# A fused attention kernel: normed tiles, a square root and projections put in another order between two attention layers

## The chip, the cores and the metric

The kernel runs on one core of one Trainium2 chip. A core has five engines that take instructions from queues of their own and wait for each other through semaphores: TensorE (PE, matrix products), VectorE (DVE, elementwise work and statistics), ScalarE (ACT, copies and activation functions), GpSimd (POOL) and SyncE (SP, which issues transfers). Products land in PSUM, which this kernel uses as eight banks of 128x512 fp32.

The metric is the device time of one execution in microseconds (us). The median of three runs of the kernel before is 2324.17 us (2321.87 to 2325.84).

## The reference

Eight images of 32x32 pixels and 384 channels go through two layers. Cut to what matters:

```python
# layer 0
x = x + conv_attention(group_norm(x))       # q, k, v; 6 heads; relative positions; softmax; projection
# layer 1
t = x.reshape(8, 1024, 384)
t = t + attention(layer_norm(t))            # one head of 384, causal
t = t + ffn(layer_norm(t))                  # sign weights, absmax quantization; changes five of eight images
```

The place of the change is the seam between the layers: the projection of layer 0 with its residual, the layer norm of each token (subtract the mean of its 384 channels, divide by the root of their variance plus 1e-5), and the query and value products of layer 1's attention:

```python
out = out @ proj_w + proj_b                 # end of layer 0's attention; x = x + out
m, s = mean(t, -1), var(t, -1)
n = (t - m) / sqrt(s + 1e-5)                # layer norm
scores = (n @ Wq) @ (n @ Wk).T              # the kernel multiplies Wq and Wk.T out once
v = n @ Wv
```

## The kernel before, in words

The images are worked on one after the other (order 5, 0 to 4, 6, 7). Within an image, the tokens lie as eight tiles of 128 (j = 0 to 7), in two halves of four. All of an image stays in SBUF between the stages.

At the seam, `attend0_fast` has left the attention output `oT` (channels on partitions). `project` multiplies one tile of it with the projection weights: three products of 384 columns, each two instructions in the trace. `begun` holds the projections of tiles 0 to 3, issued already; `more(j)` adds a projection to the residual `xt` on DVE (L975), and for j of 4 and more issues the projection first.

`normed` makes the layer norm of one half: per tile `bn_stats` and `bn_aggr` on DVE (L463, L464), then for the four tiles together an addition on DVE (L466), the square root on ACT (L467), a reciprocal on DVE (L469), and the four normed tiles `xn` on DVE (L474). It is a generator, so that its caller can do other things between its parts. `turn_normed` transposes the normed tiles on PE (L414, three transposes a tile) and copies them on ACT to `lnT` (L415).

The query and value products are made by a scheme with fewer multiplications than the plain one: a 384x384 product over 256 tokens is put together from 15 products of 128x128 blocks (`ProductSet`). There are four sets an image: queries and values of half 0 (here 1q_0 and 1v_0), then of half 1 (1q_1 and 1v_1). `sum_forms` first makes eleven sums of blocks of `lnT` on DVE (L568). `ProductSet.run` then issues the products in the order of `PROD_ORDER` into six PSUM banks A to F. Bank A gets six products and bank B five; after most of them ACT copies the partial sum out (L623, `keep`), and the next product into the same bank waits for this copy. POOL subtracts some copies from each other (L643, `PROD_COMBINE`), and DVE puts the finished blocks together (`put_queries` L1050, `put_values` L1055), which also frees a bank.

The order on an engine is the order of issue, changed where the text asks for it: `behind_of(ins)` and `tc.issue_after(ins)` put what stands under them behind the named instruction. `last_ended` carries such an instruction for DVE, `last_product` for PE. In the kernel before the text runs: `more` for tiles 0 to 6 and half 0's norm and transposes, with the statistics of half 1's first three tiles let in; half 0's forms; the last projection, its statistics and half 1's root and normed tiles; set 1q_0; half 1's transposes; 1v_0, 1q_1, 1v_1, one whole set after the other; then the scores of layer 1 (L1115).

## Time and profile before

| what | value |
|---|---|
| median of three runs | 2324.17 us |
| the profiled execution's own time | 2325.5 us |
| its span, first to last instruction | 2323.8 us |
| PE busy | 2282.9 us, 98% of the span |
| DVE busy | 1614.3 us, 69% |
| ACT busy | 1206.0 us, 52% |
| POOL busy | 525.3 us, 23% |
| mean granted PE clock | 0.992 |
| PE's waits for ACT in set 1q | 19.3 us, 8 times |

Busy time is the time in which an engine works on an instruction. The granted clock is the share of PE's full clock that the chip let through. The chain of waits follows the last instruction back to what released it. A timeline lists start, duration, engine, line and operation, and in brackets the idle time before an instruction with what ended it. In the timelines one `lsd` is the sum of variance and 1e-5 or its root, `lrs` the reciprocal, `xn` a normed tile, `pj` a projection, `pt` a transposed tile, `xf` a form and `u_1q` a copied partial sum.

### The profile page before, as it was taken

How to read it: one execution, taken by the hardware profiler on the slowest of the kernel's cores; microseconds unless marked ns; L12 is line 12 of the kernel's file. 1: busy time of each engine (PE TensorE's matmuls, PEld its weight loads, DVE VectorE, ACT ScalarE, POOL GpSimd, SP SyncE). 2: the span in 40 equal slices, each digit the busy share in tenths (PEclk: the TensorE clock that was granted, in tenths of full speed). 3: DMA queues.
4: the chain of work that ended last, by engine and by line, in shares of the span. 5: the costliest groups of instructions: out<-in, count | busy, mean ns of one | idle time of the engine just before them, and what ended most of it. 6: DMA issues, size and time to landing. Idle time of an engine off the chain costs nothing.

```text
span 2323.8 us, 30196 instructions
## 1 busy us (share of the span) xinstructions
PE 2282.9 (98%) x10739; PEld 1395.7 (60%) x10739; DVE 1614.3 (69%) x2703; ACT 1206.0 (52%) x2181; POOL 525.3 (23%) x690
## 2 busy tenths in 40 slices
PE   8999999999999999999999999999999999999998
PEld 4547554768645677547685466874477754755464
DVE  6887578775887548886468875578854788637872
ACT  4644266337663457644376543766444765326631
POOL 6412222230140401312202313013040131221310
PEclk9999999999999999999999999999999999999999
DMA  7520552040730115510308202063002362017100
GB/s 181 154 82 28 156 134 64 13 178 28 147 98 28 52 58 116 130 55 1 109 28 188 57 28 105 30 144 103 28 16 93 101 136 64 1 51 158 37 1 29
DMA packets 154137, 186.57 MB, mean 80 GB/s; under 512 B 110917, under 2 KB 123578, under 8 KB 151162
## 3 DMA queue, kind: packets, MB, share of 16 engines
q1 hardware_dynamic: 135600, 113.87, 19.9%
q0 software_dynamic: 17184, 69.22, 9.6%
q8 instruction: 88, 1.44, 0.3%
q10 hardware_dynamic: 1194, 1.45, 0.2%
q14 instruction: 71, 0.58, 0.1%
HBM read 83.24 MB, written 50.92 MB: 58 GB/s over the span
## 4 chain that ended last, share of the span: by engine, by line
PE 95%; DVE 4%; DMA 1%; issue 0%; ACT 0%; ACTq 0%; DVEq 0%
PE f_s L889 15%; PE f_av L915 14%; PE f_s L1115 8%; PE f_av L1130 8%; PE f_y L1290 7%; PE f_y L1240 7%; PE f_qk L558 5%; PE f_s L893 4%; PE f_pr_A L558 4%; PE f_pj L504 4%; PE f_pr_B L558 3%; PE f_pr_1q_A L558 2%; PE f_rel L558 2%; PE f_pr_1v_A L558 2%; PE f_pr_1v_B L558 2%; PE f_pr_1q_B L558 2%
## 5 line engine op out<-in xcount | busy, mean ns | idle before, releaser
L900 ACT ACTIVATE f_pr<-f_s 128x512 f32<-128x512 f32 x768 | 413.1, 595 | 41.4 <-PE f_s L893 36.8
L889 PE MATMUL f_s<-f_q,f_k 64*128 64x512 f32 x1536 | 399.1, 595 | 0.0
L907 DVE TENSOR_TENSOR f_sum<-f_sum,f_pr 128x1024 f32<-128x1024 f32 x288 | 362.9, 1260 | 23.5 <-DVE seen L545 0.8
L915 PE MATMUL f_av<-f_pr,f_v 128*64 128x512 f32 x1536 | 339.3, 594 | 0.0
L893 PE MATMUL f_s<-f_r,unit 64*128 64x512 f32 x768 | 308.0, 793 | 0.0
L915 PEld LDWEIGHTS f_av<-f_pr,f_v 128*64 128x64 f32 x1536 | 106.2, 137 | 196.4 <-issue 191.9
L889 PEld LDWEIGHTS f_s<-f_q,f_k 64*128 64x128 f32 x1536 | 145.9, 186 | 124.1 <-issue 66.3
L1115 PE MATMUL f_s<-f_q,f_lnT 128*128 128x512 f32 (+3 forms) x576 | 198.3, 488 | 0.0
L1130 PE MATMUL f_av<-f_v,f_pr 128*128 128x385 f32 x576 | 195.3, 486 | 0.0
L780 POOL DMA_DIRECT2D f_r<-f_far x192 | 102.1, 534 | 380.1 <-DVE f_far L774 179.9
L1130 PEld LDWEIGHTS f_av<-f_v,f_pr 128*128 128x128 f32 x576 | 108.3, 190 | 77.2 <-issue 11.5
L1124 ACT ACTIVATE f_pr<-f_s 128x512 f32<-128x512 f32 (+3 forms) x96 | 47.0, 490 | 204.3 <-DVE f_s L1120 161.5
L1115 PEld LDWEIGHTS f_s<-f_q,f_lnT 128*128 128x128 f32 x576 | 100.8, 190 | 70.3 <-issue 46.9
L1251 DVE TENSOR_REDUCE am<-f_h 128x1 f32<-128x1024 f32 (+2 forms) x80 | 71.6, 946 | 95.6 <-ACT f_h L1244 95.6
L1244 ACT ACTIVATE f_h<-f_y,biases 128x256 f32<-128x256 f32 x240 | 100.7, 471 | 67.0 <-PE f_y L1240 67.0
L905 DVE TENSOR_TENSOR f_sum<-f_pr,f_pr 128x1024 f32<-128x1024 f32 x48 | 66.5, 1385 | 92.9 <-ACT f_pr L900 92.9
L893 PEld LDWEIGHTS f_s<-f_r,unit 64*128 64x128 f32 x768 | 75.2, 187 | 89.7 <-issue 89.2
L558 PE MATMUL f_qk<-f_gnT,wq_sb 128*128 128x512 f32 x288 | 127.8, 595 | 0.0
L504 PE MATMUL f_pj<-wproj_sb,f_oT 128*128 128x384 f32 x384 | 127.3, 488 | 0.0
L1290 PE MATMUL f_y<-f_w2a,f_hilo 128*128 128x384 f32 x640 | 127.2, 341 | 0.0
L963 ACT COPY f_oT<-f_av 128x512 f32<-128x512 f32 x40 | 23.4, 585 | 193.9 <-PE f_av L915 193.9
L1290 PEld LDWEIGHTS f_y<-f_w2a,f_hilo 128*128 128x128 f32 x640 | 112.5, 188 | 3.8 <-issue 1.4
(272 smaller groups left out, 4081.2 us busy)
## 6 DMA issues: line engine op xcount, KB each, us to landing
f_far<-f_far SPq DMA_DIRECT2D x48, 512.0 KB, 4.9
f_r<-f_far SPq DMA_DIRECT2D x192, 128.0 KB, 2.8
f_r<-f_far POOLq DMA_DIRECT2D x192, 128.0 KB, 4.6
f_far<-f_far SPq DMA_DIRECT2D x192, 64.0 KB, 4.7
f_x<-in_x SPq DMA_DIRECT2D x32, 384.0 KB, 8.4
f_gnT<-in_xT SPq DMA_DIRECT2D x21, 512.0 KB, 4.6
f_w1a<-w1s POOLq DMA_DIRECT2D x5, 1536.0 KB, 6.7
f_w2a<-w2s POOLq DMA_DIRECT2D x5, 1536.0 KB, 9.1
```

The costliest lines, as they stand in the source:

```text
L504: nc.tensor.matmul(ps[:, :C], xT[:, k, ts(j, P)], w[:, k, cols], start=(k == 0), stop=(k == NC - 1))
L558: last_product[0] = nc.tensor.matmul(*args, **kw).ins
L780: put = (nc.gpsimd if i else nc.sync).dma_start(out=r(part, p).bitcast(F32).rearrange("(m i) t -> i m t", i=4)[2 * i + d], in_=pages[i][ts ...
L889: nc.tensor.matmul(sc[par], k[rows[par], p, ts(c, P)], q[rows[par], p, ts(half, 512)], start=True, stop=False)
L893: last_matmul[0] = nc.tensor.matmul(sc[par], unit[rows[par], c // 2 % 2].rearrange("i h w -> i (h w)"), r(2 * (c // 4) + c % 2, p)[rows[pa ...
L900: last_exp[0] = nc.scalar.activation(pr[:, ts(par, 512)], sc[par], AF.Exp).ins
L907: adds.append(nc.vector.tensor_tensor(total, total, pr, ALU.add).ins)
L915: last_matmul[0] = nc.tensor.matmul(av[ts(par, HD), :], v[:, c, ts(2 * p + par, HD)], pr[:, ts(par, 512)], start=(c == 0), stop=(c == NJ - 1),
L1115: last_score[0] = nc.tensor.matmul(sc[:, lo:], xT[:, c // 4, k, ts(c % 4, P)], q[:, half, k, lo:], start=(k == 0), stop=(k == NC - 1),).ins
L1130: nc.tensor.matmul(av[:, : C + 1], prs[c][:, ts(j - c, P)], v[:, c, :], start=(c == 0), stop=(c == j))
L1240: nc.tensor.matmul(ps, w1k[i // 2][:, ts(m, P)], xs[i % 2][:, half, i // 2, :], start=(i == 0), stop=(i == 2 * NC - 1))
L1290: nc.tensor.matmul(ps[:, :C], h, w, start=(i == 0), stop=(i == len(products) - 1))
```

## The change

Five edits, all in the branch for the fast path:

- `normed` gives control back after every tile's statistics and once more after the addition, so that ACT's root can be issued later than DVE's part. It also records its DVE instructions in `last_normed`.
- `more` only adds; the projections of tiles 4 to 7 are issued by a new `begin`.
- Half 0's four normed tiles are issued on DVE straight after half 0's statistics, ahead of tile 4's addition. The statistics of tiles 5 to 7 stand behind half 0's forms.
- On PE half 0's transposes stand between the projections of tiles 5 and 6 (before: between 6 and 7).
- The root of half 1 stands on ACT behind the eighth copy of set 1q_0 (before: ahead of the first). Half 1's transposes stand ahead of 1q_0's last product, and each of the first products of 1q_1 and 1v_1 stands ahead of the last product of the set before.

In the built program these are the only differences of order on PE; DVE, ACT and POOL differ in the same stretch alone, and SP does not differ. Which PSUM bank and which page of SBUF a tile gets is different in this stretch: half 1's third and fourth transposed tiles lie in the banks that D and E of 1q_0 had, in both kernels, and so wait for DVE's first two `put_queries`.

```diff
@@ normed
             for i, j in enumerate(js):
-                if i == 3:
-                    yield
                 st = pools.small.tile([P, 6], F32, tag="lst", name=f"lst_{name}_{j}")
                 nc.vector.bn_stats(st, xt[:, j, :])
-                nc.vector.bn_aggr(mv[:, i, :], st)
+                last_normed[0] = nc.vector.bn_aggr(mv[:, i, :], st).ins
+                yield
             sd = pools.small.tile([P, 4], F32, tag="lsd", name=f"lsd_{name}_{half}")
-            nc.vector.tensor_scalar_add(sd, mv[:, :, 1], 1e-5)
+            last_normed[0] = nc.vector.tensor_scalar_add(sd, mv[:, :, 1], 1e-5).ins
+            yield
             nc.scalar.activation(sd, sd, AF.Sqrt)
...
@@ attend0_fast
+            def begin(j):
+                begun[j] = project(wproj_sb, slice(0, C), oT, j, f"pj_{b}_{j}")
+
             def more(j):
-                ps = begun[j] if j < 4 else project(wproj_sb, slice(0, C), oT, j, f"pj_{b}_{j}")
-                nc.vector.tensor_tensor(xt[:, j, :], ps, xt[:, j, :], ALU.add)
+                nc.vector.tensor_tensor(xt[:, j, :], begun[j], xt[:, j, :], ALU.add)
...
@@ attention1
-            for j in range(7):
-                more(j)
-            layer_norm_T(xt, xT, 0, f"1_{b}")
             if pools.fast:
+                begin, more = more
+                for j in range(4):
+                    more(j)
+                *_, (tiles, _) = normed(xt, 0, f"1_{b}")
+                tiles = list(tiles)
+                begin(4)
+                norm = normed(xt, 1, f"1_{b}")
+                with behind_of(last_normed[0]):
+                    more(4)
+                    next(norm)
                 last_ended[0] = last_normed[0]
-                norm = normed(xt, 1, f"1_{b}")
-                next(norm)
+                begin(5)
+                turn_normed(xT, 0, tiles)
+                begin(6)
+                begin(7)
                 forms = forms_of(0)
                 with behind_of(last_ended[0]):
-                    more(7)
+                    for j in range(5, NJ):
+                        more(j)
+                        next(norm)
+                    next(norm)
+                last_ended[0] = last_normed[0]
+                of_q, of_v = products(0, forms)
+                of_q.run(10)
+                with behind_of(last_ended[0]), behind_of(of_q.last_copy):
                     tiles, _ = next(norm)
                     tiles = list(tiles)
                 last_ended[0] = last_normed[0]
-                first = products(0, forms)
-                next(first)
+                of_q.run(4, put_queries(0))
                 with behind_of(last_product[0]):
                     turn_normed(xT, 1, tiles)
                 last_product[0] = last_transpose[0]
+                of_q.run(1)
                 forms = forms_of(1)
-                next(first, None)
-                second = products(1, forms)
-                next(second)
+                of_v0, (of_q, of_v) = of_v, products(1, forms)
+                of_v0.run(14, put_values(0))
+                of_q.run(1)
+                of_v0.run(1)
+                of_q.run(13, put_queries(1))
+                of_v.run(1)
+                of_q.run(1)
                 queries_ended[0] = last_ended[0]
-                next(second, None)
+                of_v.run(14, put_values(1))
```

More of the change, by code (lines that the diff above doesn't have):

```diff
@@ L970, in attend0_fast @@
             with behind_last():
-                begun = [project(wproj_sb, slice(0, C), oT, j, f"pj_{b}_{j}") for j in range(4)]
+                begun = {j: project(wproj_sb, slice(0, C), oT, j, f"pj_{b}_{j}") for j in range(4)}
+            def begin(j):
+                begun[j] = project(wproj_sb, slice(0, C), oT, j, f"pj_{b}_{j}")
             def more(j):
-                ps = begun[j] if j < 4 else project(wproj_sb, slice(0, C), oT, j, f"pj_{b}_{j}")
-                nc.vector.tensor_tensor(xt[:, j, :], ps, xt[:, j, :], ALU.add)
-            return xt, more
+                nc.vector.tensor_tensor(xt[:, j, :], begun[j], xt[:, j, :], ALU.add)
+            return xt, (begin, more)
         def attend0_general(residual, b, q, k, r, v, later):
@@ L1025, in attend0_general @@
             pipelined([(j, h) for j in range(NJ) for h in range(NH)], scores, values)
-            return xt, lambda j: None
+            return xt, None
         def attention1(xt, more, b, between, start):
@@ L1045, in forms_of, with put_queries, put, put_values @@
                 return sum_forms(f"1_{b}_{half}", lambda k, n: xT[:, half, k, ts(1 - n, 256)], 256, nc.vector, True)
-            def products(half, forms):
-                def put_queries(ps, kept, p, n, op):
+            def put_queries(half):
+                def put(ps, kept, p, n, op):
                     return nc.vector.tensor_tensor(q[:, half, p, ts(1 - n, 256)], ps, kept, op).ins
-                def put_values(ps, kept, p, n, op):
+                return put
+            def put_values(half):
+                def put(ps, kept, p, n, op):
                     ps, kept = (t.rearrange("t (j c) -> t j c", j=2) for t in (ps, kept))
@@ L1055, in put_values, with products @@
                     return nc.vector.tensor_tensor(v[:, j : j + 2, ts(p, P)], ps, kept, op).ins
-                ProductSet(f"1q_{b}_{half}", forms, w1f[:, :, 0, :], 256, eng=nc.gpsimd).run(N_PROD, put_queries)
-                yield
-                of_v = ProductSet(
+                return put
+            def products(half, forms):
+                return ProductSet(f"1q_{b}_{half}", forms, w1f[:, :, 0, :], 256, eng=nc.gpsimd), ProductSet(
                     f"1v_{b}_{half}", forms, w1f[:, :, 1, :], 256, lambda x: [x[:, ts(j, P)] for j in range(2)], eng=nc.gpsimd
                 )
-                of_v.run(N_PROD, put_values)
-            for j in range(7):
-                more(j)
-            layer_norm_T(xt, xT, 0, f"1_{b}")
             if pools.fast:
+                begin, more = more
[8 more added lines that the diff above has]
+                    next(norm)
                 last_ended[0] = last_normed[0]
-                norm = normed(xt, 1, f"1_{b}")
-                next(norm)
+                begin(5)
+                turn_normed(xT, 0, tiles)
+                begin(6)
+                begin(7)
                 forms = forms_of(0)
                 with behind_of(last_ended[0]):
-                    more(7)
+                    for j in range(5, NJ):
[6 more added lines that the diff above has]
+                with behind_of(last_ended[0]), behind_of(of_q.last_copy):
                     tiles, _ = next(norm)
@@ L1081, in attention1 @@
                 last_product[0] = last_transpose[0]
+                of_q.run(1)
                 forms = forms_of(1)
-                next(first, None)
-                second = products(1, forms)
-                next(second)
+                of_v0, (of_q, of_v) = of_v, products(1, forms)
[5 more added lines that the diff above has]
+                of_q.run(1)
                 queries_ended[0] = last_ended[0]
-                next(second, None)
+                of_v.run(14, put_values(1))
             else:
-                more(7)
+                layer_norm_T(xt, xT, 0, f"1_{b}")
                 layer_norm_T(xt, xT, 1, f"1_{b}")
```

## The prediction

> **What bounds the kernel now.** I read the chain of waits first, then PE's waits, then the timelines of the seam between the layers in the fifth image, and the granted clock in windows.

> Chain of waits, shares by engine; PE's longest wait:

> ```profile
> PE 95%; DVE 4%; DMA 1%; issue 0%; ACT 0%; ACTq 0%; DVEq 0%
> ...
> PE f_pr_1q_A L558 <- ACT f_u_1q L623: 19.3, 8, 2.4
> ```

> PE is the bound. What can be won is PE's idle or slow time, and its largest wait comes once an image, in set 1q_0. PE's timeline there (fifth image):

> ```profile
> 1364.91 2.10 PE L504 MATMUL f_pj<-wproj_sb,f_oT 128*128 128x384 f32 x6
> 1366.85 0.59 PE L558 MATMUL f_pr_1q_A<-f_xf,w1f 128*128 128x256 f32 x2
> 1367.71 0.70 PE L558 MATMUL f_pr_1q_B<-f_xf,w1f 128*128 128x256 f32 x2 [0.27 <-DVE f_xf L568]
> 1368.50 0.70 PE L558 MATMUL f_pr_1q_C<-f_xf,w1f 128*128 128x256 f32 x2
> 1371.61 0.70 PE L558 MATMUL f_pr_1q_A<-f_xf,w1f 128*128 128x256 f32 x2 [2.41 <-ACT f_u_1q L623]
> ```

> The second product of A waits for ACT's copy of the first. ACT stands at half 1's root, which waits for DVE (both timelines):

> ```profile
> 1370.89 0.17 DVE L466 TENSOR_SCALAR lsd<-lmv 128x4 f32<-128x4 f32 x1
> ...
> 1371.10 0.20 ACT L467 ACTIVATE lsd<-lsd 128x4 f32<-128x4 f32 x1 [5.34 <-DVE lsd L466]
> 1371.21 0.35 ACT L623 COPY f_u_1q<-f_pr_1q_A 128x256 f32<-128x256 f32 x1
> ```

> The wait has a second price. In the fourth image the products behind it start 0.85 us apart; in the fifth 0.43. PE's timeline and the windows (the seventh number, counts in brackets aside, is the clock):

> ```profile
> 1057.35 1.22 PE L558 MATMUL f_pr_1q_A<-f_xf,w1f 128*128 128x256 f32 x2 [2.41 <-ACT f_u_1q L623]
> 1058.36 1.06 PE L558 MATMUL f_pr_1q_B<-f_xf,w1f 128*128 128x256 f32 x2
> ...
> 1050.00:1060.00 10.00, 7.23 (x26) 4.76 (x25) 8.28 (x24) 3.24 (x10) 0.10 (x1) 0.81 0.00 0
> 1060.00:1070.00 10.00, 9.97 (x58) 8.59 (x57) 4.96 (x13) 5.23 (x14) 2.86 (x5) 0.85 0.00 1
> ```

> From the first projection to the first score takes 50.03, 51.39, 51.44, 51.37, 48.56, 48.55, 50.24 and 50.13 us in the eight images. Above 48.56 that is 13.2 us in all: the slow clock's cost. Ahead of 2310 us every 10 us window with a clock below 1.00 lies at this seam.

> [...] two forms take 1.70 us beside two POOL subtractions, 0.88 without:

> ```profile
> 1368.02 0.88 DVE L568 TENSOR_TENSOR f_xf<-f_xf,f_lnT 128x256 f32<-128x256 f32 x2
> ...
> 1381.59 1.70 DVE L568 TENSOR_TENSOR f_xf<-f_xf,f_lnT 128x256 f32<-128x256 f32 x2
> ```

> For `xn` beside POOL this trace has no case (all 104 take 0.456 to 0.481 us).

> **The change, part by part**, on the fifth image's clock. Instructions and transfers stay the same in number; SP's and POOL's order too, so no queue is passed.

> *Loss before.* Set pitch is 0.43 us a product for queries, 0.447 for values. From 1q_0's first product (1366.85) to the first score (1398.51) are 31.66 us. Needed: 15x0.4315 + transposes 1.32 + 15x0.4467 + 15x0.4315 + 14x0.4467 = 27.2. The loss is 4.43: B 0.43 and C 0.36 late for their forms, the wait 2.68, refilling 0.11, and 0.29, 0.27, 0.29 where the last product of 1q_0, 1v_0, 1q_1 waits for the copy just before it. Eight times 4.43 is 35.4 us; with the clock 48.7 us are at stake.

> *Half 0 early.* A root that is ready comes 0.44 us after its addition (1370.89 to 1371.33): reciprocal at 1359.84, xn 0 at 1360.05, pitch 0.38, so xn 3 ends at 1361.65 (before: 1363.3). Projections take 1.95 us each, so PE reaches the transposes at 1361.65: no wait, and 1q_0 begins at 1366.85 as before, since the same work is only reordered. ACT's copies follow the transposes by 0.53 and last 1.63: 1362.2 to 1363.8. Tile 4's addition and statistics end at 1362.9, so the forms start at about 1363.1 instead of 1365.09, take 4.4, and B and C don't wait: 0.79 won.

> *Root behind the eighth copy.* The first copies follow their products by 0.63, as in the later sets, so 2.68 + 0.11 go. What is late next? The forms end at 1367.5; three additions (pitch 0.47), three statistics and aggregations follow, in the row's pitches: `lsd` at 1370.9. The eighth copy starts at 1366.85 + 9x0.4315 + 0.64 = 1371.4, the root at 1371.63: 0.5 us of cover. Behind it stand copies nine (due 1371.80) and ten: not delayed. Reciprocal 1371.86, xn 4 at 1372.08, pitch 0.40, xn 7 at 1373.27, first put (D) 1373.67 to 1374.10.

> *The new wait.* PE would begin half 1's transposes at 1366.85 + 14x0.4315 = 1372.9. The third needs D's bank at 1373.55, but gets it at 1374.13: 0.58 us. POOL's subtraction for n3 (0.72 us) starts at 1371.82, just before xn 4: if it blocks it, 0.46 more. That for n6 falls on xn 5 to 7: up to 0.72 more. So 0.58 to 1.76; I take 1.3, one block and half of the other, plus 0.11 for refilling: 1.4. Queued behind D are E, F, C, B and A: the fourth transpose (E) follows 0.33 later without more wait, C is back before 1v_0's third product.

> *Set overlap.* One foreign product (0.43) stands before each last product, and covers 0.27 and 0.29; the transposes cover 1q_0's 0.29. Half 1's forms begin about 0.9 us later against 1v_0, but are wanted only 6.2 us after its start: covered.

> *Sum.* 4.43 - 1.4 = 3.03 an image, 24.2 us. If the slow clock goes too, 13.2 more: 37.5. The profiled execution's 2325.5 (span 2323.8) becomes 2288.0; the median stands 1.3 lower: **2287 us**.

> **Rivals.**
> (a) *The seam stays in the slow clock.* The new wait stands among transposes: from 1372.9 to 1375.6 PE has about 1.3 us of transposes and 1.4 of idleness. [...] For it: six of eight images after 2.41 us. Against: 1.4 us of idleness is little over half of that. All kept: 2324.2 - 24.2 = 2300; half kept 2293.
> (b) *Half 1's statistics are late.* DVE works 9.70 us of the ten from 1360 to 1370, and its cover is 0.5 us. 1.5 us late would push root, copies nine and ten and the transposes by 1 us more, and the clock goes slow: 2300 + 8 = 2308.
> (c) *Slower.* The root now stands ahead of copies nine and ten, so every delay of `lsd` past 1371.6 stops bank B, and PE, one for one. It decides where `lsd` comes 6.1 us (48.7 / 8) after its slot, at 1377.5; at 7 us the time is 2324 + 7 = 2331. The page has no DVE wait near that.
> (d) *No change:* only if new waits eat all; the order on ACT does show the root moved.

> **How the numbers follow.** Likeliest case 0.60: 2287, its own range 2280 to 2293 (wait 0.58 to 2.0). (a) 0.24; (b) 0.10; (c) 0.04; (d) 0.02. Faster than 0.2%, about what a measurement of this kernel can tell from no change, are the first three: 0.94. No residual at all would be 2324.2 - 48.7 = 2275.5, no block 2281: low end 2278. High end: slow clock kept and a wait of 2.0, 2304.

> **What would show it.** Right: no wait of 1q's A for the copies; granted clock 1.00 at the seam; a wait of about 1 us at half 1's third transpose, put down to DVE's put; first projection to first score about 45.5 us in each image. Wrong: distances of 0.85 behind the transposes (a); a wait of B in 1q_0 for copy nine and ACT idle for `lsd` (b, c); xn of 0.46 us beside POOL (then 2283).

## The result and the profile after

| | before | after |
|---|---|---|
| median | 2323.02 us (2321.37 to 2325.84, 4 runs) | 2286.43 us (2285.97 to 2286.72, 4 runs) |
| span of the profiled execution | 2323.8 us | 2284.7 us |
| mean granted PE clock | 0.992 | 0.999 |
| first product to first score, per image | 31.66 us at full clock, up to 34.54 | 28.45 or 28.46 us |
| the same, sum of eight images | 266.55 us | 227.63 us |

The ratio is 0.9841, with a 95% interval of 0.9824 to 0.9858. The kernel became faster by 36.6 us; 2287 was forecast. The seam accounts for the gain: 266.55 - 227.63 = 38.9 us, against 39.1 us of difference between the spans. Of these, 8 x (31.66 - 28.45) = 25.7 us are waits that went, net of the new one, and 266.55 - 8 x 31.66 = 13.3 us are the slow clock, which after doesn't show in any image's seam.

After's chain of waits by engine:

```profile
PE 98%; DVE 1%; DMA 1%; ACTq 0%; issue 0%; ACT 0%; DVEq 0%
```

PE's share rose from 95% to 98% and DVE's fell from 4% to 1%. The longest entry of PE's waits (total, times, longest):

```profile
PE f_pt L414 <- DVE f_q L1051: 7.8, 8, 1.0
```

The wait of 19.3 us for ACT's copies is gone. In its place PE waits 0.97 us an image at half 1's transposes. PE's timeline in the fifth image, whose first product of 1q_0 is now at 1343.87 (before: 1366.85):

```profile
1343.87 0.59 PE L558 MATMUL f_pr_1q_A<-f_xf,w1f 128*128 128x256 f32 x2
1344.30 0.59 PE L558 MATMUL f_pr_1q_B<-f_xf,w1f 128*128 128x256 f32 x2
...
1345.16 0.59 PE L558 MATMUL f_pr_1q_A<-f_xf,w1f 128*128 128x256 f32 x2
...
1349.91 0.86 PE L414 MATMUL f_pt<-ident,f_xn 128*128 128x128 f32 x6
1351.75 0.88 PE L414 MATMUL f_pt<-ident,f_xn 128*128 128x128 f32 x6 [0.97 <-DVE f_q L1051]
1352.46 0.60 PE L558 MATMUL f_pr_1q_A<-f_xf,w1f 128*128 128x256 f32 x2
```

From A's first product to its second are 1.29 us, three steps of 0.43; before they were 4.76. The transposes of tiles 4 and 5 start at 1349.91; those of tiles 6 and 7 could follow 0.66 us later but start 1.84 us later: a loss of 1.18 us, of which the profile counts 0.97 as idle.

ACT, DVE and POOL in the same stretch of after:

```profile
1347.86 0.44 DVE L465 TENSOR_SCALAR lsd<-lmv 128x4 f32<-128x4 f32 x1
1348.39 0.37 ACT L623 COPY f_u_1q<-f_pr_1q_A 128x256 f32<-128x256 f32 x1 [0.49 <-PE f_pr_1q_A L558]
1348.66 0.21 ACT L467 ACTIVATE lsd<-lsd 128x4 f32<-128x4 f32 x1
1348.84 0.73 POOL L643 TENSOR_TENSOR f_u_1q<-f_u_1q 128x256 f32<-128x256 f32 x1 [0.56 <-ACT f_u_1q L623]
1348.90 0.18 DVE L469 RECIPROCAL lrs<-lsd 128x4 f32<-128x4 f32 x1 [0.60 <-ACT lsd L467]
1349.11 2.25 DVE L474 TENSOR_SCALAR f_xn<-f_x,lmv,lrs 128x384 f32<-128x384 f32 x4
...
1350.19 0.96 POOL L643 TENSOR_TENSOR f_u_1q<-f_u_1q 128x256 f32<-128x256 f32 x1 [0.62 <-POOL f_u_1q L643]
...
1351.28 0.41 DVE L1051 TENSOR_TENSOR f_q<-f_pr_1q_D,f_u_1q 128x256 f32<-128x256 f32 x1
```

ACT now runs the root behind a copy, not ahead of one. The four normed tiles take 2.25 us beside POOL's two subtractions, and D's put (DVE's last step for bank D, which frees the bank) comes behind them; PE starts again 0.06 us after its end (1351.69).

### The profile page after: what moved, and what is told of

Read it like the earlier page. It is cut to its first block, busy times and chain, and to the rows that moved or that the text cites. A ratio compares the mean times of both kernels' runs of the same rounds, so it can differ in the third digit from the quotient of the medians.

```text
span 2284.7 us, 30195 instructions
## 1 busy us (share of the span) xinstructions
PE 2258.8 (99%) x10739; PEld 1387.6 (61%) x10739; DVE 1629.5 (71%) x2703; ACT 1210.5 (53%) x2181; POOL 527.2 (23%) x690
## 4 chain that ended last, share of the span: by engine, by line
PE 98%; DVE 1%; DMA 1%; ACTq 0%; issue 0%; ACT 0%; DVEq 0%
PE f_s L889 15%; PE f_av L915 14%; PE f_s L1139 8%; PE f_av L1154 8%; PE f_y L1314 7%; PE f_y L1264 7%; PE f_pj L504 5%; PE f_qk L558 5%; PE f_s L893 4%; PE f_pr_A L558 4%; PE f_pr_B L558 3%; PE f_rel L558 2%; PE f_pr_1v_A L558 2%; PE f_pr_1q_A L558 2%; PE f_pr_1v_B L558 2%; PE f_pr_1q_B L558 1%
## 5 line engine op out<-in xcount | busy, mean ns | idle before, releaser
L558 PE MATMUL f_qk<-f_gnT,wq_sb 128*128 128x512 f32 x288 | 127.8, 595 | 0.0
L504 PE MATMUL f_pj<-wproj_sb,f_oT 128*128 128x384 f32 x384 | 127.3, 488 | 0.0
```

Of the source, the lines that this page charges most:

```text
L504: nc.tensor.matmul(ps[:, :C], xT[:, k, ts(j, P)], w[:, k, cols], start=(k == 0), stop=(k == NC - 1))
L558: last_product[0] = nc.tensor.matmul(*args, **kw).ins
```

## The experiments

The theory: the gain is the root's move with the slow clock it caused, plus the earlier forms and the covered last products, less a new wait that hangs on DVE's chain from root to D's put. The rivals: the gain came from the other edits, or transposes and idleness together may keep the slow clock. Half 0's earlier tiles were not tried alone; what they do is read from the timeline. "Per image" below is the time from the first product of 1q_0 to the first score, at full clock; after has 28.45 us.

| run | median us | ratio to before (95%) | per image, us | slow clock in all, us |
|---|---|---|---|---|
| root back | 2314.05 | 0.9938 (0.9922 to 0.9955) | 30.73 | 9.2 |
| root alone | 2295.77 | 0.9866 (0.9849 to 0.9882) | 29.63 | 0 |
| last product first | 2283.75 | 0.9813 (0.9797 to 0.9829) | 28.07 | 0 |
| banks before puts | 2285.88 | 0.9821 (0.9804 to 0.9837) | 28.45 | 0 |
| whole later sets | 2291.36 | 0.9847 (0.9828 to 0.9866) | 29.03 | 0 |
| root behind tenth copy | 2291.46 | 0.9849 (0.9829 to 0.9868) | 29.05 | 0 |
| no subtractions | 2281.66 | 0.9805 (0.9786 to 0.9824) | 27.85 | 0 |
| put in the gap | 2280.29 | 0.9801 (0.9782 to 0.9820) | 27.74 | 0 |
| every wait | 2281.01 | 0.9820 (0.9804 to 0.9836) | 27.74 | 0 |
| long wait | 2325.36 | 1.0005 (0.9996 to 1.0014) | 29.91 | 9.8 |
| long wait, seam only | 2306.45 | 0.9915 (0.9893 to 0.9938) | 29.90 | 9.6 |
| shorter wait, seam only | 2301.99 | 0.9893 (0.9869 to 0.9916) | 29.15 to 29.98 | 8.2 |

The slow clock's share is the sum of the eight images less the same images at full clock, and 0 where the trace grants the full clock at every seam; in the two runs with the long wait 0.7 us for a later wait for DVE in one image are left out. The kernel before has 31.66 us and 13.3 us in these two columns. Runs that are close are compared by their seams, since the medians of the kernel before that they were measured against lie between 2323.0 and 2327.7.

**The root put back**

```diff
-                of_q.run(10)
-                with behind_of(last_ended[0]), behind_of(of_q.last_copy):
+                with behind_of(last_ended[0]):
...
-                of_q.run(4, put_queries(0))
+                of_q.run(14, put_queries(0))
```

> The changed kernel with one edit undone: half 1's root stands ahead of set 1q_0's first copy again; half 0's earlier tiles, the transposes and the shared set ends stay. Theory (the root's place carries most of the gain): the first copy of A waits for half 1's statistics again, some 3 us an image, where the changed kernel shows the wait of 1.18 us between half 1's transposes instead; net 1.5 to 2.5 us an image, 12 to 20 us, and the slow clock of 1q_0 returns in most images, 8 to 15 us more: 2307 to 2321 us, with a wait of 1q's A for the copies in all 8 images. Rival (the gain came from half 0's earlier tiles and the shared ends, the root's place is a detail): 2287 to 2295 us, full clock at the seam.

2314.05 us. PE's longest wait in this run:

```profile
PE f_pr_1q_A L558 <- ACT f_u_1q L623: 26.0, 8, 3.3
```

The old wait is back, and longer (3.25 against 2.41 us), since the products now begin earlier against half 1's statistics, which stand behind the forms. An image costs 2.28 us more than in after, 18.2 us in all, and the slow clock returns in five images, 9.2 us. The other edits without the root are worth 31.66 - 30.73 = 0.93 us an image.

**The root alone**, in the kernel before: half 1's root behind the eighth copy, nothing else.

```diff
+                of_q.run(10)
+                yield of_q
...
+                first = products(0, forms)
+                of_q = next(first)
+                with behind_of(last_ended[0]), behind_of(of_q.last_copy):
```

> The kernel before with one edit made: half 1's root behind the eighth copy of set 1q_0; half 0's tiles, the transposes' place behind the whole set and the separate sets stay as before. Theory: the wait of A for the copies (2.68 us start to start and 0.11 of refilling, an image) goes, the slow clock with it (13 us in all); left are B's and C's late forms (0.79 an image), the waits of the three last products (0.85 an image), and a wait of up to 0.6 us at half 1's transposes: 2290 to 2294 us. Rival (the edits only work together, since without the earlier half 0 the statistics come too late for the new slot): copies nine and ten wait for the root, the clock goes slow again, 2305 us or more.

2295.77 us. 29.63 us an image is 2.03 less than before, 16.2 us, and all 13.3 us of slow clock are gone: 29.5 of the 38.9 us. The rival falls, copies nine and ten do not wait. The time lies just above the range expected (2294). PE waits 0.29 us at the transposes, less than in after, because 1q_0's last product stands ahead of them here. The next run asks about that.

**1q_0's last product ahead of the transposes**

```diff
-                of_q.run(4, put_queries(0))
+                of_q.run(5, put_queries(0))
                 with behind_of(last_product[0]):
                     turn_normed(xT, 1, tiles)
                 last_product[0] = last_transpose[0]
-                of_q.run(1)
```

> The changed kernel with set 1q_0's last product (B) ahead of half 1's transposes again, as in the kernel before. Theory A (the transposes wait for the bank of D, freed by DVE at a fixed time): the product of 0.43 us stands in front of the wait and shortens it, so the sets end 0.43 us earlier less what B itself waits for its copy, at most 0.29; gain 0.15 to 0.43 us an image, 1 to 3.5 us: 2283 to 2285 us, and the wait at the third transpose falls from 1.18 to about 0.75 us. Theory B (as the prediction had it, the transposes cover B's wait of 0.29 us, and the rest is unchanged): 0.29 us an image is lost, 2288 to 2289 us.

2283.75 us, 0.38 us an image less than after: theory A. PE's timeline:

```profile
1347.92 0.59 PE L558 MATMUL f_pr_1q_B<-f_lnT,w1f 128*128 128x256 f32 x2
1348.55 0.70 PE L558 MATMUL f_pr_1q_A<-f_xf,w1f 128*128 128x256 f32 x2
1349.09 0.82 PE L414 MATMUL f_pt<-ident,f_xn 128*128 128x128 f32 x6
1350.19 0.88 PE L414 MATMUL f_pt<-ident,f_xn 128*128 128x128 f32 x6 [0.29 <-DVE f_q L1051]
```

The product waits 0.20 us for its copy, but the wait among the transposes falls from 1.18 to 1.10 - 0.66 = 0.44 us. D's bank comes at a time that PE doesn't set; work in front of it is free. So this part of the change, which saved the last product's wait, cost more than it saved.

**Banks claimed before the puts**: the transposes are issued ahead of DVE's puts, so that C's put is the first.

```diff
-                of_q.run(4, put_queries(0))
+                of_q.run(4)
...
-                of_q.run(1)
+                of_q.run(1, put_queries(0))
```

> The changed kernel with half 1's transposes claiming their PSUM banks before DVE's last steps of set 1q_0 are given out, so that the first of those steps is C's instead of D's and another bank is waited for. Theory (the wait is for a DVE step that stands behind the four normalised tiles, whichever it is): the third transpose still waits, now for C's step, which also needs POOL's last subtraction, so 0.2 us less to 0.5 us more an image: 2284 to 2290 us. Rival (the wait is an accident of which bank is claimed, and another order removes it): the wait of 1.18 us goes or falls below 0.5 us, 2277 to 2281 us.

2285.88 us, the same 0.97 us of idleness in all images. DVE's first put is C's, right behind the normed tiles as D's was. Which bank it frees is of no account; the wait is for the first put behind the tiles.

**Later sets whole**

```diff
-                of_v0.run(14, put_values(0))
-                of_q.run(1)
-                of_v0.run(1)
-                of_q.run(13, put_queries(1))
-                of_v.run(1)
-                of_q.run(1)
+                of_v0.run(15, put_values(0))
+                of_q.run(15, put_queries(1))
...
-                of_v.run(14, put_values(1))
+                of_v.run(15, put_values(1))
```

> The changed kernel with the sets 1v_0, 1q_1 and 1v_1 whole again, one after the other; the root's place, half 0's tiles and the transposes stay. Theory (one foreign product ahead of a set's last product covers that product's wait for its copy): 0.27 and 0.29 us come back, 0.56 us an image, 4.5 us: 2290 to 2292 us. Rival (the next set's own wait takes it over, the overlap is worth nothing): 2285 to 2288 us.

2291.36 us. 29.03 - 28.45 = 0.58 us an image: the 0.27 and 0.29 us of the two later last products are back. The overlap is worth 4.6 us.

**The root behind the tenth copy**

```diff
-                of_q.run(10)
+                of_q.run(13)
...
-                of_q.run(4, put_queries(0))
+                of_q.run(1, put_queries(0))
```

> The changed kernel with half 1's root two copies later, behind the tenth copy of set 1q_0, so that the normalised tiles of half 1 and the wait among its transposes come later. The copies before it finish 1.3 us after the eighth. Theory (PE's wait at the transposes follows the root, and what is idle there doesn't slow the clock by itself): the wait grows from 1.18 us to 2.2 to 2.6 us, 2294 to 2299 us, full clock. Rival ([...] at this size the clock goes slow as it did after the old wait of 2.4 us): 5 to 13 us more, 2301 to 2311 us, with products 0.85 us apart behind the transposes in several images.

2291.46 us, less than either expectation. The normed tiles begin 1.29 us later after the first product than in after, but an image loses only 0.60 us. PE's timeline:

```profile
1352.18 0.59 PE L558 MATMUL f_pr_1q_B<-f_lnT,w1f 128*128 128x256 f32 x2
1353.87 0.94 PE L414 MATMUL f_pt<-ident,f_xn 128*128 128x128 f32 x6 [1.10 <-DVE f_xn L474]
1354.99 0.94 PE L414 MATMUL f_pt<-ident,f_xn 128*128 128x128 f32 x6 [0.18 <-DVE f_xn L474]
1355.76 0.60 PE L558 MATMUL f_pr_1q_A<-f_xf,w1f 128*128 128x256 f32 x2
```

POOL's third subtraction is over before the tiles begin, so they take 1.89 instead of 2.25 us, and PE now waits for the tiles themselves, not for a put. From the end of B's step (1352.18 + 0.43) to the next product lie 3.15 us with nothing but transposes and waits, more than the 2.68 us lost before, yet the clock is full in all eight images. So the transposes don't count as idleness, or not in full. What a longer wait does was left open, since the idle pieces are only 1.10 and 0.18 us.

**No subtractions in 1q_0**

```diff
-                    if name in PROD_COMBINE:
+                    if name in PROD_COMBINE and not (self.name.startswith("1q_") and self.name.endswith("_0")):
```

> The changed kernel without POOL's four subtractions in set 1q_0 of each image, a part of the computation left out. Theory (POOL's subtractions lengthen half 1's four normalised tiles from 1.65 to 2.25 us, and these set PE's wait at the third transpose): the four take about 1.65 us, the wait falls from 1.18 to about 0.6 us, 4.5 us less: 2281 to 2283 us. Rival (the tiles are slow for another reason, or the wait is set by something else): 2.25 us and 2285 to 2288 us as in the changed kernel.

2281.66 us. The timeline of this run, DVE and PE:

```profile
1345.48 0.17 DVE L465 TENSOR_SCALAR lsd<-lmv 128x4 f32<-128x4 f32 x1
...
1346.73 1.65 DVE L474 TENSOR_SCALAR f_xn<-f_x,lmv,lrs 128x384 f32<-128x384 f32 x4
...
1348.77 0.88 PE L414 MATMUL f_pt<-ident,f_xn 128*128 128x128 f32 x6 [0.42 <-DVE f_q L1051]
```

Without POOL the tiles take 1.65 us, as half 0's do in after, and an image costs 0.60 us less. The tiles begin 5.24 us after the first product here and in after, so the difference is their own length. About half of the new wait is POOL in DVE's way.

**D's put in DVE's gap**, on top of the last product first. While ACT makes the root, DVE is idle for 0.60 us, and D's put takes 0.41.

```diff
-                of_q.run(10)
+                of_q.run(7, put_queries(0))
+                of_q.final = None
+                of_q.run(3)
```

> The kernel of the run with set 1q_0's last product ahead of the transposes (2283.75 us), with one step of DVE moved: D's last step stands between half 1's addition for the root and its reciprocal, where DVE is idle for 0.6 us, instead of behind the four normalised tiles. Theory (the third transpose waits for nothing but D's bank): the wait of 0.44 us start to start goes down to 0.1 us or less, now at the fourth transpose for E's step, 2.5 to 3 us in all: 2280 to 2282 us. Rival (D's step delays the reciprocal and the tiles by as much as it saves): 2283 to 2286 us.

2280.29 us, the best of all kernels here: 0.71 us an image less than after. Its timeline:

```profile
1345.84 0.42 DVE L1051 TENSOR_TENSOR f_q<-f_pr_1q_D,f_u_1q 128x256 f32<-128x256 f32 x1 [0.43 <-PE f_pr_1q_A L558]
...
1346.18 0.17 DVE L469 RECIPROCAL lrs<-lsd 128x4 f32<-128x4 f32 x1
1346.38 2.10 DVE L474 TENSOR_SCALAR f_xn<-f_x,lmv,lrs 128x384 f32<-128x384 f32 x4
...
1347.76 1.66 PE L414 MATMUL f_pt<-ident,f_xn 128*128 128x128 f32 x12
```

All twelve transposes run in one piece. D's put delays the tiles a little: they begin 5.39 us after the first product, where they began after 5.24 us in the run with the last product first. But they take 2.10 us instead of 2.25, so they end at the same time, 7.49 us after the first product in both runs.

**Every wait at once**: in addition the root behind the seventh copy, and the last product between the transposes of tiles 5 and 6.

```diff
-                of_q.run(3)
+                of_q.run(1)
...
+                    turn_normed(xT, 1, tiles[:2])
+                last_product[0] = last_transpose[0]
+                of_q.run(1)
+                with behind_of(last_product[0]):
+                    turn_normed(xT, 1, tiles[2:], at=2)
```

> A candidate for the best order of the seam: as the run with D's step in DVE's gap (2280.29 us), but half 1's root stands behind the seventh copy of set 1q_0 (0.4 us earlier), and set 1q_0's last product stands between the transposes of half 1's second and third tile. Theory (what is left at the seam are waits of 0.2 us for the last copy and 0.24 us among the transposes, and a product in between covers them): 0.2 to 0.4 us an image less, 1.6 to 3.2 us: 2277 to 2279 us. Rival (the transposes now come sooner than the second normalised tile, and PE waits for it instead): 2279.5 to 2282 us, with a wait of half 1's transposes for the tiles.

2281.01 us and the same 27.74 us an image, which is the rival's time but not its reason: PE waits 0.22 us at the transposes again, though for a put (E's) and not for a tile. What the last product saves goes there.

**A long wait among the transposes**: half 1's last normed tile is computed several times over, first five times.

```diff
+                    for _ in range(5 if half == 1 and i == 3 and pools.fast else 1):
```

> The changed kernel with half 1's last normalised tile computed five times over by DVE instead of once, so that the wait at half 1's third transpose grows by four instructions of 0.40 us, to some 2.6 us of idleness in one piece among the transposes, more than the 2.41 us after which the kernel before fell into the slow clock. Rival (a) of the prediction ([...] a wait among them is at least as good as the old one for slowing the clock): 2286.4 + 12.8 = 2299.2 us and 8 to 16 us of slow clock on top, 2307 to 2315 us, products 0.85 us apart behind the transposes in several images. The other way (a wait at this place doesn't slow the clock at all): 2298 to 2301 us, clock full.

2325.36 us, more than either expectation. The edit also reached the second layer's norm of half 1 in five images, where PE waited 2.43 us each: of the 38.3 us of span above after's, 249.82 - 227.63 = 22.2 lie at the seam. The slow clock is back there. PE's timeline in the fifth image:

```profile
1373.85 0.52 PE L414 MATMUL f_pt<-ident,f_xn 128*128 128x128 f32 x3 [2.05 <-DVE f_xn L475]
1374.20 1.01 PE L559 MATMUL f_pr_1q_A<-f_xf,w1f 128*128 128x256 f32 x2
```

The product behind a wait of 2.05 us takes 1.01 us (0.60 in after). To be free of the other five places, the edit was made at the seam alone, with five and with three repeats:

```diff
-                    for _ in range(5 if half == 1 and i == 3 and pools.fast else 1):
+                    for _ in range(5 if half == 1 and i == 3 and name.startswith("1_") else 1):
```

> The last run's lengthened tile turned out to lie in the second layer's norm of five images too. Here only the seam's last tile of half 1 is computed five times over. From that run's trace the seam alone: 28.45 us from the first product to the first score becomes 29.91 us by the wait itself (8 x 1.46 = 11.7 us) and 249.82 - 8 x 29.91 = 10.5 us by the slow clock. If a wait among transposes slows the clock as the old wait did: 2286.4 + 11.7 + 10.5 = 2308.6 us, 2304 to 2313. If the slow clock there was an effect of the waits elsewhere: 2297 to 2300 us.

2306.45 us, as worked out, and 20.0 us more than after. With 2.05 us of idleness in each image, the slow clock costs 1.5 to 1.7 us in six images and nothing in two; one of those two has a later wait for DVE instead, 0.7 us. At the seam the eight images take 249.51 us, 21.9 more than in after: 11.6 by the wait, 9.6 by the clock, 0.7 by the later wait.

> The same with the tile computed three times over: 2 x 0.40 = 0.8 us less than five times, so the wait itself costs some 8 x 0.66 = 5.3 us and PE is idle for about 1.25 us in one piece, with 0.2 us just before it. If what slows the clock is an idle stretch of two microseconds or so: full clock, 2290 to 2294 us. If any idleness among transposes beyond the changed kernel's 0.97 us does it: 8 to 13 us more, 2299 to 2305 us.

2301.99 us. The wait was longer than worked out: 1.26 us in the first image, 1.53 in the second, 2.08 in the seventh, 1.73 in five, because DVE stood still ahead of D's put, for 0.18 us in the second image, 0.38 in the fifth and 0.73 in the seventh, for a reason the profile doesn't show. So the run doesn't decide cleanly between its two expectations, but its images are a scale. The second and the fifth:

```profile
429.38 0.55 PE L414 MATMUL f_pt<-ident,f_xn 128*128 128x128 f32 x3 [1.53 <-DVE f_q L1052]
429.76 0.99 PE L559 MATMUL f_pr_1q_A<-f_xf,w1f 128*128 128x256 f32 x2
...
1362.02 0.55 PE L414 MATMUL f_pt<-ident,f_xn 128*128 128x128 f32 x3 [1.73 <-DVE f_q L1052]
1362.40 0.60 PE L559 MATMUL f_pr_1q_A<-f_xf,w1f 128*128 128x256 f32 x2
```

1.53 us slow, 1.73 us full: the length of the piece alone doesn't decide. Longest idle piece at the seam and images with a slow clock, over the runs where it is 0.97 us or more: 0.97 us none of 24 (after and two runs), 1.10 none of 8, 1.26 none of 1, 1.53 one of 1, 1.73 three of 5, 2.05 twelve of 16 (two runs), 2.08 one of 1, 2.41 six of 8 (before), 3.25 five of 8 (the root put back).

The place of the piece matters too, as can be read from the traces' record of the clock. Within each run all its changes lie whole multiples of 3.4133 us apart (88 changes in 14 traces, to within 0.002 us); in before the clock is halved, for instance, from 185.86 to 189.28 us, one such step, and from 428.21 to 435.04, two. So in these runs the clock changes at the borders of windows of 3.413 us alone, and the borders lie differently against the program in each image. Each line below is one such window: its start and end, its length, PE's busy time, in brackets the number of instructions, and the clock. The first three are of this run (second image, the window after it, fifth image), the last two of the fourth image of the run with the root put back:

```profile
426.41:429.83 3.42, 1.69 (x13) 1.00 0.02 5
429.83:433.24 3.41, 3.41 (x16) 0.50 0.00 0
...
1358.25:1361.67 3.42, 1.85 (x12) 1.00 0.00 0
...
1047.26:1050.67 3.41, 1.77 (x8) 1.00 0.00 0
1050.67:1054.09 3.42, 1.81 (x8) 1.00 0.00 0
```

In the second image all idleness, 1.73 us, lies in one window, and the next window has half the clock. In the fifth a border cuts the wait: 1.57 us lie in one window and the rest in the next, and the clock stays full. The wait of 3.25 us with the root put back is cut into 1.64 and 1.61 us, and the clock stays full too. Over all windows of the 14 traces that began at full clock, from where the record of the clock begins (in before at 11.79 us), none with up to 1.65 us of idleness was followed by a slow one, and every one with 1.99 us or more was; of the 15 between 1.69 and 1.97 us, eight were (PE's ends are modelled, so the idle times are not exact). So in these runs it was about half a window of idleness that slowed the clock, and where the wait fell decided whether it filled half of one. What decides between 1.69 and 1.97 us stays open.

## Why the prediction was right

**The bound and the stake.** Right. PE bounds the kernel, and the time went where it was looked for: 38.9 of 39.1 us lie between the first product and the first score.

**Half 0 early.** Right to the hundredths: the forms were to start 3.75 us ahead of 1q_0's first product (1363.1 against 1366.85) and start 3.76 us ahead (1340.11), and B and C keep the pitch of 0.43 us. This and the covered last products are the 0.93 us that the run with the root put back keeps, although its wait is longer.

**Root behind the eighth copy.** Right. The root alone, in the kernel before, takes away the wait and the whole slow clock. `lsd` came 3.99 us after the first product (4.05 worked out), xn 4 after 5.24 (5.23). One size was off: the addition for `lsd` took 0.44 us, not 0.17, beside POOL; without POOL's subtractions it is 0.17 again. So the cover was 1348.66 - 1348.30 = 0.36 us, not 0.5. Rivals (b) and (c) had no room: copies nine and ten follow at once.

**The new wait.** Right in place, cause and nearly in size: 1.18 us of 1.3 taken. The block by POOL is 2.25 - 1.65 = 0.60 us, where one block of 0.46 and half of another, 0.36, were taken. The half was a guess between none and all. The run without subtractions wins just these 0.60 us, and the 0.58 us that it leaves are the wait that was worked out without any block.

**Set overlap.** Right for 1v_0 and 1q_1, 0.58 us where 0.27 + 0.29 were worked out. Wrong in what it said of 1q_0: "the transposes cover 1q_0's 0.29" is true of that wait, but the step booked it as a gain and did not ask what the same product is worth in front of the wait for D's bank. There it would have saved 0.38 us an image net. The error sat inside the 1.4 us of the new wait, so the sum did not show it.

**The sum.** 3.03 us an image were worked out, 31.66 - 28.45 = 3.21 measured; 24.2 and 25.7 us. First projection to first score takes 45.34 or 45.35 us in every image (about 45.5). The difference of 0.18 us an image is the new wait, 1.18 us for 1.3, and the refilling behind it, 0.05 us for 0.11.

**The clock and rival (a).** The likeliest case held, 13.3 us where 13.2 were at stake. Its argument, that 1.4 us is little over half of 2.41, is right only in part: it compared lengths of waits, while the runs with the lengthened tile and the windows of the traces show that here the idleness within one window of 3.413 us decided. By this measure the case had room: a window at after's seams holds at most 0.98 us of idleness, and the 1.3 us that were forecast would have stayed below 1.69, the least that slowed the clock. Of rival (a), one half is borne out: waits of 1.53 to 2.08 us among the transposes did slow the clock in most images, for 8 to 10 us a run. The other half, that the transposes beside a wait add to the idleness, is not shown. With the root behind the tenth copy, a window in the fourth image (1043.59 to 1047.00) holds 1.28 us of idleness, 1.71 of transposes and only 0.42 of products, and the clock stays full; before, 1.69 us of idleness with nothing but products beside it slowed the clock. Whether transposes weigh in some smaller part stays open.

## What to carry to other kernels

An instruction that waits for another engine should stand behind everything that is ready before its input, and its price is to be counted twice: the wait itself (2.41 us an image here), and the PE clock that was halved for 3.41 or 6.83 us behind it in six of before's eight images. For the clock it was PE's idleness within a window of 3.413 us that counted: with 1.65 us or less, in one piece or in several, it stayed full. Where a wait ends at a time that the waiting engine doesn't set, move its own ready work in front of it (0.38 us an image here), and look for a gap on the engine that is waited for (0.33 us more): both together beat the change by 6 us. A covered wait is no gain if the cover was taken from in front of a longer one.
